# A GRU and an expert-choice layer on one core: the order of the head, and the place of a count in the tail

## The chip, the cores and the metric

The kernel runs on one core of a Trainium2 chip. The metric is the device time of one execution in microseconds (us). Before the change the median of five runs is 1196.7 us (1193.42 to 1199.73).

The engines are named as the profile names them. PE is TensorE (PEld its weight loads), DVE is VectorE, ACT is ScalarE and POOL is GpSimd. SP is SyncE, which issues transfers. SPq, ACTq and POOLq are transfers that these engines issue.

## The reference

`x` is [16, 256, 512]: 16 sequences, 256 steps, 512 features. A GRU runs over the steps from the state `cond_2048`:

```python
def cell(h, x):
    gi = x @ W_ih + b_ih
    gh = h @ W_hh + b_hh
    i_r, i_z, i_n = jnp.split(gi, 3, axis=-1)
    h_r, h_z, h_n = jnp.split(gh, 3, axis=-1)
    r = jax.nn.sigmoid(i_r + h_r)
    z = jax.nn.sigmoid(i_z + h_z)
    n = jnp.tanh(i_n + r * h_n)
    h_new = (1.0 - z) * n + z * h
```

All 4096 states then go through a router with 16 experts. Each expert chooses the 256 tokens with its highest softmax weight; all experts share one matrix.

```python
S = jax.nn.softmax(xf @ router_w + router_b, axis=-1)
G, idx = jax.lax.top_k(S.T, k)               # k = 256 tokens for each expert
out = jnp.einsum('ekh,hd->ekd', xf[idx], expert_w) + expert_b
y = zeros.at[idx.reshape(-1)].add((G[..., None] * out).reshape(-1, h))
```

The result is `x + y`. As the experts share a matrix, a token's `y` is its product with `expert_w` plus `expert_b`, times the sum of its chosen weights, its gate.

## The kernel before

**Sizes and tiles.** The steps come in 32 groups of 8 (`TG`), and a group has four pairs of steps. 512 columns are four chunks of 128 (`KC`). A gate's 512 columns are computed as four quadrants of 32 partitions, so one group of four matmuls fills 128 partitions. A float32 matmul shows as two instructions in the profile.

**The head.** SyncE and ScalarE load the two weight matrices, each by three gates in the order r, n, z and in halves (L229). GpSimd issues, in an order written out by hand: the biases (L274), the x of group 0 into `xa0` (L237, eight transfers of 16 partitions by four pairs), a memset and the start state `cond` (L279, into a part of the tile `xs`). SyncE then loads the x of group 1 into `xa1`, which shares its buffer with `xa0`, and `expert_w`, `router_w` and the two broadcast biases (L284 to L287). Eight transfers of SyncE and ScalarE together are in flight at a time, and eight of GpSimd.

On TensorE, `begin_sums` (L110) writes zero products into a PSUM bank, which opens its sums. There are banks `ra`, `hn` and `zz` for each of two pairs of steps (index 0 and 1). Bias products follow into both sets (L302), and the set of index 1 is copied to SBUF as `bias` and `nb` (L311 to L313), from which later pairs are preset (L384 to L386). VectorE transposes the x of group 0 in one instruction (`turn_x`, L253) and the start state (L316, L321). Then `x_part` (L398) adds the products with `W_ih` for pairs 0 and 1: first r and n of both pairs, then z of both.

**The steps.** For each step, `h_part` (L411) adds the products with `W_hh`: r and n by halves of the depth, then z. ScalarE and VectorE make the new state (L468 to L508). VectorE transposes each new `hs` half by half, and TensorE starts the next step when the first half is there. The order of all engines in the steps is written out by hand. The x products of the next pair (L398) and the expert products of earlier groups (L365) fill TensorE's waits. `turn_x` for the next group is called at the fourth step of a group (L524), and `load_x` and `load_xa` issue x transfers on SyncE behind a small GpSimd copy.

**The late groups.** The odd groups and group 30 are `late_groups`, 17 of them, with eight parts of products each (L138, a part is four matmuls, eight instructions). `expert_for(n)` emits the next n parts on TensorE. A late group's sum is begun two groups ahead: ScalarE presets its PSUM buffer with `expert_b` (L158), and five buffers rotate. Late groups that end before the gate is known are copied to SBUF (L175); the others stay in PSUM until `store`.

**The tail.** Each expert's threshold is found bit by bit on VectorE (`count`, L585, and L600 to L608), with late parts between the count products on TensorE. After 17 bits, an exact selection among the highest eight remaining values (L667 to L684) gives `kth`. Four products (`sum_weights`, L628) give each token's gate, L632. Then 32 `store`s follow (L638, L641): 15 groups whose sums are ready, and then the 17 late groups, each after its parts. After the third store, the kernel counts once more with `kth` (L702 to L707), to learn whether each expert has exactly 256 tokens. If not, a general path is run behind a branch (L709); on these inputs it is not. The order of TensorE, ScalarE and VectorE is by hand here too, so an instruction that waits holds up all that its engine has behind it.

Of the kernel before, what the change touches and what calls it, by code (L numbers as in the profile page):

```python
# [18 lines left out]
def kernel(  # L19
# [166 lines left out]
    with (  # L186
# [63 lines left out]

        def turn_x(g, xa):
            t = xtp.tile([P, TG // 2, P], F32, name="xt")
            nc.vector.transpose(  # L253
                t.rearrange("p q (c r) -> p q c r", c=KC), xa.rearrange("p q (i c) -> p q c i", c=KC)
            )
            xT[g] = t

# [3 lines left out]
        xa1 = new_xa()  # L261
        with tc.manual_schedule(engines={ET.SP, ET.Activation, ET.Pool}):
            for i, gate in enumerate((0, 2, 1)):
                load_rows(wih[:, :, i, :], w_ih[:, gate * D : (gate + 1) * D], "(p c) n -> p c n")
            for gate in (0, 2, 1):
                load_rows(whh[:, :, gate, :], w_hh[:, gate * D : (gate + 1) * D], "(c p) n -> p c n")

            for dst, src in (
                (b_raw[0:1], b_ih.rearrange("(o g d) -> o g d", o=1, d=D)),
                (b_raw[1:2], b_hh.rearrange("(o g d) -> o g d", o=1, d=D)),  # L270
                (b_n, b_hh[2 * D :].rearrange("(o d) -> o d", o=1)),
                (b_r, router_b.rearrange("(o e) -> o e", o=1)),
            ):
                nc.gpsimd.dma_start(out=dst, in_=src)  # L274
            for j in range(KC):
                load_xa(0, xa0, j, (nc.gpsimd, nc.gpsimd))
            nc.gpsimd.memset(c0, 0.0)
            for j in range(KC):
                nc.gpsimd.dma_start(  # L279
                    out=c0[QD * j : QD * j + B, :].rearrange("b (c i) -> b c i", c=KC), in_=columns(cond, j)  # L280
                )
            for j in range(KC):
                load_xa(1, xa1, j, (nc.sync, nc.sync))
# [6 lines left out]

        for i in range(2):
            for bank in (ra[i].rearrange("p g d -> p (g d)"), hn[i], zz[i]):
                begin_sums(bank)
            for dst, rows in (
# [6 lines left out]
                for j in range(KC):  # L301
# [8 lines left out]
                    )  # L310
        nc.vector.tensor_copy(bias[:, 0:2, :], ra[1])  # L311
        nc.vector.tensor_copy(bias[:, 2, :], zz[1])
        nc.vector.tensor_copy(nb, hn[1])  # L313

        turned = gp.tile([P, P], F32, name="nT")
        nc.vector.transpose(turned, c0)  # L316

        def of_step(ap, odd):
            return ap.rearrange("p (c q b) -> p c q b", q=2, b=B)[:, :, odd, :]

        nc.vector.tensor_copy(hs[:, :, 0, :], of_step(turned, 0))  # L321

# [97 lines left out]

        turn_x(0, xa0)
        make_masks()
        xa_next = xa1
        for z in (False, True):
            for p in range(2):
                for k in range(KC):
                    x_part(p, k, z)

# [7 lines left out]
        with tc.manual_schedule(engines={ET.PE, ET.Activation, ET.DVE, ET.Pool, ET.SP}):  # L436
            units = []
            for s in range(T):
# [79 lines left out]
                if odd and p + 2 < T // 2:  # L518
                    preset(p + 2)
                if apart and c == 0:  # L520
                    less_max(g - 1, hn[(p + 1) % 2][:, P:])
# [44 lines left out]
    with (  # L566
# [86 lines left out]
        with tc.manual_schedule(engines={ET.PE, ET.Activation, ET.DVE}):  # L653
# [25 lines left out]
            nc.tensor.matmul(all_most, same_f, spread.rearrange("p h n -> p (h n)"), start=True, stop=True)  # L679
            expert_for(2)  # L680
            room = above(counts)
# [6 lines left out]
            for q in range(QG):  # L688
                part = slice(q * P, (q + 1) * P)
                nc.vector.scalar_tensor_tensor(at_least[:, part], sT[:, part], kth, sT[:, part], ALU.is_ge, ALU.mult)  # L690
                sum_weights(q, pg)
            gate = gate_of(pg)

            gated.append(True)
            for i, g in enumerate([g for g in range(NG) if g not in late_groups] + late_groups):
                while g in late_groups and g not in late_done:
                    expert_for(1)
                store(g, late_sums.get(g, wide(g)), gate)
                if i == 2:

# [93 lines left out]
```

## Time and profile before

| | |
|---|---|
| median of five runs | 1196.7 us |
| the profiled execution | 1194.21 us, its span 1192.4 us |
| mean granted TensorE clock | 0.996 |
| last bias product ends, first x product starts | 11.93, 17.92 us |
| first product of step 0, of step 1 | 24.78, 28.87 us |
| gate sums end, late parts go on | 1144.83, 1148.32 us |
| late parts end | 1186.55 us |

How to read it: times are microseconds from the span's start. In a timeline line stand the start, the time, the engine, the line of the kernel, the operation, the tiles (out, then in), the shapes, the count of instructions put together, and in brackets how long the engine had been idle and what ended this. A line with a count over one can have holes inside. In a line of a window the columns are the stretch and its length, the busy time of PE, PEld, DVE, ACT and POOL with their counts, the granted TensorE clock (1.00 is full), the busy share of the DMA engines, and GB/s. In the head the clock column reads 1.00 throughout, though the first x products (17.9 to 21.3) start every 0.43 us by groups of four and the later ones every 0.22.

### The profile page before, as it was taken

What the parts mean: (1) busy time and instruction counts of PE and PEld (TensorE: products, weight loads), DVE (VectorE), ACT (ScalarE), POOL (GpSimd) and SP (SyncE); (2) the same over time, 40 slices, a digit from 0 to 9 for tenths busy, and PEclk for the clock granted to TensorE, in tenths of its full rate; (3) what the DMA queues carried; (4) which work ended last, traced back from release to release, by engine and by line L of the source; (5) the groups of instructions that cost most, each with busy time, mean ns of one, the idle gap of its engine ahead of it and who ended that gap; (6) DMA issues with size and microseconds to landing.
All of it is one profiled execution on the core that took longest, in us unless ns stands there. A gap on an engine that the chain in (4) does not pass through costs nothing.

```text
span 1192.4 us, 80820 instructions
## 1 busy us (share of the span) xinstructions
PE 1154.9 (97%) x36477; PEld 1047.7 (88%) x36477; DVE 684.9 (57%) x3868; ACT 319.4 (27%) x1430; POOL 99.4 (8%) x412
## 2 busy tenths in 40 slices
PE   5999999999999999999999999999999999999788
PEld 3899999999999999999999999999899999999444
DVE  2555655565565656555565556565565556555682
ACT  0222222223222222222222222222222222223210
POOL 3000000000000000000000000000000000000000
PEclk9999999999999999999999999999999999999999
DMA  8000000000000000000000000000000000000044
GB/s 274 25 23 20 20 18 23 20 20 20 20 20 20 19 21 20 20 20 20 21 20 21 18 20 19 22 19 21 20 20 18 22 20 20 18 14 13 2 144 143
DMA packets 48349, 38.09 MB, mean 32 GB/s; under 512 B 7744, under 2 KB 40064, under 8 KB 48000
## 3 DMA queue, kind: packets, MB, share of 16 engines
q1 hardware_dynamic: 45856, 29.43, 8.5%
q8 instruction: 287, 4.70, 1.6%
q10 hardware_dynamic: 1632, 3.15, 0.8%
q14 instruction: 62, 0.51, 0.1%
q0 software_dynamic: 512, 0.31, 0.1%
HBM read 24.47 MB, written 8.39 MB: 28 GB/s over the span
## 4 chain that ended last, share of the span: by engine, by line
PE 91%; DVE 5%; DMA 1%; issue 1%; ACT 1%; POOL 0%; DVEq 0%; ACTq 0%; POOLq 0%
PE ra L411 19%; PE hn L411 19%; PE ra L398 17%; PE zz L411 17%; PE zz L398 10%; PE pe L365 5%; PE pe L138 4%; DVE nT L494 1%; DVE t L485 1%; DVE zT L497 1%; DVE ge L585 1%; ACT n L489 1%; DMA xs<-in_L_cond_b_hh_dram 1%; DMA xs<-in_cond_dram 0%; DVE hs L508 0%
## 5 line engine op out<-in xcount | busy, mean ns | idle before, releaser
L411 PE MATMUL ra<-whh,hs 128*16 128x128 f32 (+1 forms) x8192 | 345.1, 273 | 7.7 <-DVE zT L497 6.1
L411 PE MATMUL hn<-whh,hs 128*16 128x128 f32 (+1 forms) x8192 | 345.0, 273 | 0.0
L485 DVE TENSOR_TENSOR t<-r,hn 128x64 f32<-128x64 f32 x512 | 90.5, 218 | 360.5 <-PE hn L411 357.0
L398 PE MATMUL ra<-wih,xt 128*32 128x256 f32 x4096 | 286.0, 381 | 7.1 <-DVE xt L253 6.0
L411 PE MATMUL zz<-whh,hs 128*16 128x128 f32 (+1 forms) x8192 | 285.4, 273 | 0.1
L411 PEld LDWEIGHTS ra<-whh,hs 128*16 128x16 f32 (+1 forms) x8192 | 242.7, 103 | 17.7 <-issue 6.8
L411 PEld LDWEIGHTS hn<-whh,hs 128*16 128x16 f32 (+1 forms) x8192 | 256.8, 103 | 0.2
L411 PEld LDWEIGHTS zz<-whh,hs 128*16 128x16 f32 (+1 forms) x8192 | 239.8, 103 | 1.5 <-issue 0.9
L468 ACT ACTIVATE r<-ra 128x128 f32<-128x128 f32 x256 | 71.0, 277 | 595.8 <-PE ra L411 595.8
L398 PEld LDWEIGHTS ra<-wih,xt 128*32 128x32 f32 x4096 | 157.0, 110 | 40.7 <-DVE xt L253 6.4
L489 ACT ACTIVATE n<-t 128x64 f32<-128x64 f32 x512 | 103.5, 249 | 193.1 <-DVE t L487 192.9
L398 PE MATMUL zz<-wih,xt 128*32 128x128 f32 x4096 | 146.1, 273 | 1.0 <-issue 0.9
L398 PEld LDWEIGHTS zz<-wih,xt 128*32 128x32 f32 x4096 | 128.6, 110 | 16.3 <-issue 3.1
L494 DVE STREAM_TRANSPOSE nT<-n 128x64 f32<-128x64 f32 x512 | 100.6, 234 | 57.2 <-ACT n L489 56.8
L497 DVE STREAM_TRANSPOSE zT<-zs 128x64 f32<-128x64 f32 x512 | 121.7, 238 | 0.7 <-ACT zs L490 0.4
L508 DVE TENSOR_TENSOR hs<-v,nT 128x32 f32<-128x32 f32 x512 | 101.8, 199 | 21.7
L505 DVE TENSOR_TENSOR v<-u,zT 128x32 f32<-128x32 f32 x512 | 104.6, 204 | 8.8
L365 PE MATMUL pe<-ewr,ht 128*32 128x136 f32 (+1 forms) x1920 | 107.8, 276 | 0.0
L487 DVE TENSOR_TENSOR t<-t,ra 128x64 f32<-128x64 f32 x512 | 88.6, 214 | 0.1
L365 PEld LDWEIGHTS pe<-ewr,ht 128*32 128x32 f32 x1920 | 75.7, 110 | 10.9 <-issue 0.2
L500 DVE TENSOR_TENSOR u<-hs,nT 128x32 f32<-128x32 f32 x512 | 78.3, 153 | 0.0
L138 PE MATMUL pe<-ewr,ht 128*32 128x256 f32 x1088 | 66.4, 394 | 0.0
(109 smaller groups left out, 494.3 us busy)
## 6 DMA issues: line engine op xcount, KB each, us to landing
xs<-in_x_dram SPq DMA_DIRECT2D x128, 64.0 KB, 2.3
out_dram<-xs SPq DMA_DIRECT2D x32, 256.0 KB, 3.6
xa<-in_x_dram SPq DMA_DIRECT2D x248, 32.0 KB, 1.9
wih<-in_L_cond_W_ih_dram SPq DMA_DIRECT2D x3, 512.0 KB, 8.1
wih<-in_L_cond_W_ih_dram ACTq DMA_DIRECT2D x3, 512.0 KB, 9.0
whh<-in_L_cond_W_hh_dram SPq DMA_DIRECT2D x3, 512.0 KB, 13.8
whh<-in_L_cond_W_hh_dram ACTq DMA_DIRECT2D x3, 512.0 KB, 14.5
ewr<-in_L_ffn_expert_w_dram SPq DMA_DIRECT2D x1, 1024.0 KB, 5.7
```

The lines of the kernel that those rows point to most:

```text
L138: nc.tensor.matmul(pe[q, cols], ht[:, g, k, q], ewr[:, k, E:][:, cols], start=False, stop=(k == KC - 1), tile_position=(0, QD * j), skip_g ...
L365: nc.tensor.matmul(pe[quadrant(j), at : at + w], ht[:, g, k, quadrant(j)], ewr[:, k, src : src + w], start=(k == 0), stop=(k == KC - 1), t ...
L398: nc.tensor.matmul(dst, lhs, rhs, start=False, stop=(k == KC - 1), tile_position=(0, QD * j), skip_group_check=True)
L411: nc.tensor.matmul(dst[quadrant(j, m)], lhs, columns(whh[:, k, gate_, :], j), start=False, stop=(k == KC - 1), tile_position=(0, QD * j), ...
L485: nc.vector.tensor_tensor(t[half], r[:, cols], hn[p % 2][:, cols], ALU.mult)
L487: nc.vector.tensor_tensor(t[half], t[half], ra[p % 2][:, 1, cols], ALU.add)
L489: nc.scalar.activation(n[half], t[half], AF.Tanh)
L494: nc.vector.transpose(nT[half], n[half])
L497: nc.vector.transpose(zT[half], zs[:, halves[half][1]])
L500: nc.vector.tensor_tensor(u[half], hs[:, halves[half][2], slot(s), :], of_step(nT[half], odd), ALU.subtract)
L505: nc.vector.tensor_tensor(v[half], u[half], of_step(zT[half], odd), ALU.mult)
L508: nc.vector.tensor_tensor(hs[:, halves[half][2], slot(s + 1), :], v[half], of_step(nT[half], odd), ALU.add)
```

## The change

*In the head.* The x of group 0 is loaded pair by pair, four transfers of 32 partitions to a pair (`load_pair`). GpSimd issues those of pair 0 ahead of the biases and those of pair 1 behind `cond`; SyncE issues those of pairs 2 and 3 behind the weights and ahead of `xa1`. `turn_x` can transpose some pairs only: pair 0 and pair 1 separately in the head, pairs 2 and 3 together after step 1. On TensorE all sums are begun first, then 22 rounds of zero products go into a spare bank (`keep_clock`), then come the x products of pair 0, two rounds, the biases of both sets, two rounds, and the x products of pair 1. The order of TensorE and VectorE in this stretch is now by hand, with the start state's transpose last on VectorE.

*In the tail.* Three late parts are called earlier: one more after the selection's product, and one after each second gate product. The count for the general path moves from behind the third store to behind that of index 28 (`NG - 4`), the 14th late group; three stores remain after it.

```diff
-        def turn_x(g, xa):
-            t = xtp.tile([P, TG // 2, P], F32, name="xt")
+        def turn_x(g, xa, pairs=slice(0, TG // 2)):
+            if g not in xT:
+                xT[g] = xtp.tile([P, TG // 2, P], F32, name="xt")
             nc.vector.transpose(
-                t.rearrange("p q (c r) -> p q c r", c=KC), xa.rearrange("p q (i c) -> p q c i", c=KC)
-            )
-            xT[g] = t
+                xT[g][:, pairs, :].rearrange("p q (c r) -> p q c r", c=KC),
+                xa[:, pairs, :].rearrange("p q (i c) -> p q c i", c=KC),
+            )
...
+            def load_pair(p, qs):
+                for j in range(KC):
+                    qs[j % 2].dma_start(
+                        out=xa0[quadrant(j), p, :],
+                        in_=x[:, 2 * p : 2 * p + 2, j * P : (j + 1) * P].rearrange("b o d -> o b d"),
+                    )
...
+            load_pair(0, (nc.gpsimd, nc.gpsimd))
             for dst, src in (
...
-            for j in range(KC):
-                load_xa(0, xa0, j, (nc.gpsimd, nc.gpsimd))
             nc.gpsimd.memset(c0, 0.0)
...
+            load_pair(1, (nc.gpsimd, nc.gpsimd))
+            for p in range(2, TG // 2):
+                load_pair(p, (nc.sync, nc.sync))
             for j in range(KC):
                 load_xa(1, xa1, j, (nc.sync, nc.sync))
...
+        idle = ps_m.tile([P, D], F32, name="idle", tag="pe")
+        def keep_clock(n):
+            for _ in range(n):
+                begin_sums(idle)
+
+        with tc.manual_schedule(engines={ET.PE, ET.DVE}):
+            for i in range(2):
+                for bank in (ra[i].rearrange("p g d -> p (g d)"), hn[i], zz[i]):
+                    begin_sums(bank)
+            keep_clock(22)
+            turn_x(0, xa0, slice(0, 1))
+            for z in (False, True):
+                for k in range(KC):
+                    x_part(0, k, z)
+            keep_clock(2)
+            biases(1)
+            biases(0)
+            keep_clock(2)
+            nc.vector.tensor_copy(bias[:, 0:2, :], ra[1])
+            nc.vector.tensor_copy(nb, hn[1])
+            nc.vector.tensor_copy(bias[:, 2, :], zz[1])
+            turn_x(0, xa0, slice(1, 2))
+            for z in (False, True):
+                for k in range(KC):
+                    x_part(1, k, z)
+            nc.vector.transpose(turned, c0)
+            nc.vector.tensor_copy(hs[:, :, 0, :], of_step(turned, 0))
         make_masks()
         xa_next = xa1
-        for z in (False, True):
-            for p in range(2):
-                for k in range(KC):
-                    x_part(p, k, z)
...
+                if s == 1:
+                    turn_x(0, xa0, slice(2, TG // 2))
...
-            expert_for(2)
+            expert_for(3)
             room = above(counts)
...
                 sum_weights(q, pg)
+                if q % 2:
+                    expert_for(1)
...
-                if i == 2:
+                if i == NG - 4:
```

`biases(i)` holds the bias products that stood in a loop before; `begin_sums`, `x_part` and the bias products themselves are unchanged.

## The prediction

> **What bounds the kernel now.** I read the page's busy shares first, then the chain of waits, and then the timeline of the two ends, because the diff touches only the head, the first steps and the tail.
>
> ```profile
> PE 1154.9 (97%) x36477; PEld 1047.7 (88%) x36477; DVE 684.9 (57%) x3868; ACT 319.4 (27%) x1430; POOL 99.4 (8%) x412
> PE 91%; DVE 5%; DMA 1%; issue 1%; ACT 1%; POOL 0%; DVEq 0%; ACTq 0%; POOLq 0%
> ```
>
> The 256 steps between the ends are TensorE's and stay as they are. What can move is the time until TensorE begins step 0, and the holes it has after the last step. The head, from the timeline:
>
> ```profile
> 3.40 2.06 POOL L237 DMA_DIRECT2D xa<-in_x_dram  x4
> 8.08 1.07 PE L302 MATMUL ra<-xs,ones 2*32 2x128 f32 x16 [6.09 <-DMA xs<-in_L_cond_b_hh_dram]
> 11.76 0.51 POOL L279 DMA_DIRECT2D xs<-in_cond_dram  x1
> 16.78 1.08 DVE L253 STREAM_TRANSPOSE xt<-xa 128x512 f32<-128x512 f32 x1 [4.50 <-DMA xs<-in_cond_dram]
> 17.92 5.29 PE L398 MATMUL ra<-wih,xt 128*32 128x256 f32 x64 [5.99 <-DVE xt L253]
> 23.03 1.92 PE L398 MATMUL zz<-wih,xt 128*32 128x128 f32 x64
> 23.67 0.31 SPq L237 DMA_DIRECT2D xa<-in_x_dram  x1
> 24.78 0.61 PE L411 MATMUL ra<-whh,hs 128*16 128x128 f32 x16
> 28.87 0.64 PE L411 MATMUL ra<-whh,hs 128*32 128x128 f32 x16 [1.30 <-DVE zT L497]
> ```
>
> TensorE idles from 11.93 (the last bias product) to 17.92 for the transposed x of group 0, whose transfers GpSimd issues behind the biases. It then needs 7 us for the x products of pairs 0 and 1. The SyncE line at 23.67 dates the last weights: eight of the SyncE and ScalarE transfers are in flight at a time, and by the queue's waits this seventh xa transfer waited for whh's third gate (z), its SyncE half; the ScalarE half had landed by 24.03. The tail:
>
> ```profile
> 1143.65 1.18 PE L628 MATMUL pg<-row_of,at_least 128*128 128x8 f32 x8
> 1147.09 0.74 DVE L585 TENSOR_SCALAR_CACHE_REDUCE ge<-sT,kth 128x512 bf16<-128x512 f32 x1
> 1147.89 0.16 PE L702 MATMUL n<-cnt,same_h 128*128 128x1 f16 x1 [3.06 <-DVE ge L585]
> 1148.32 38.23 PE L138 MATMUL pe<-ewr,ht 128*32 128x256 f32 x680
> 1160.51 2.76 DVE L638 SCALAR_TENSOR_TENSOR xs<-pe,gate,xs 128x512 f32<-128x512 f32 x4
> 1186.68 0.75 DVE L638 SCALAR_TENSOR_TENSOR xs<-pe,gate,xs 128x512 f32<-128x512 f32 x1 [2.70 <-DMA out_dram<-xs]
> ```
>
> TensorE is idle from 1144.83 to 1148.31, but for one count product: the count stands in its order before the remaining 85 late parts (680 instructions), and those end the kernel. The hole also costs clock; the granted clock is the column before the last two:
>
> ```profile
> 1147.00:1148.00 1.00, 0.11 (x1) 0.00 (x0) 0.84 (x3) 0.00 (x0) 0.00 (x0) 0.83 0.80 193
> 1148.00:1151.00 3.00, 2.75 (x30) 1.27 (x33) 2.65 (x6) 0.00 (x0) 0.00 (x0) 0.50 0.57 202
> 1151.00:1152.00 1.00, 1.00 (x24) 0.54 (x20) 1.00 (x3) 0.00 (x0) 0.00 (x0) 0.96 0.92 242
> 1188.50:1189.00 0.50, 0.00 (x0) 0.00 (x0) 0.00 (x0) 0.00 (x0) 0.00 (x0) 0.62 0.67 139
> 31.50:35.00 3.50, 2.25 (x84) 2.04 (x80) 1.66 (x11) 1.52 (x7) 0.17 (x1) 1.00 0.10 27
> ```
>
> Half clock runs from 1147.66 (0.83 over that 1 us) to 1151.08. The late parts lose half of 1148.31 to 1151.08, 1.4 us.
>
> **The head, step by step.** GpSimd's sixteen transfers stay sixteen, at about 0.5 us of issue each and eight in flight. Pair 0's four now go first, 1.33 to 3.4; with the 6.1 us to landing of this queue's xa row they land by 9.0. The transpose of a quarter costs 0.31 (row of the 128x128 turn of c0), so 9.3. wih's gates r and n have landed by 10.31 (that ScalarE issue waited for one), the third by about 13.3, one more interval of 3.3. The 22 zero products are 88 instructions; one group of four 512-wide starts 0.22 us after the other late in the run, 0.43 at half clock, so they end between 7 and 11.4; at worst they delay x by 1 us and this is hidden by what follows. Pair 0's x products are half of 64 and 64 instructions: at full clock 1.75 + 0.88, ending near 14 behind wih's third gate. The biases (3.85 at the slow pace of 8.08 to 11.93) and four more zero products (0.9 to 1.7) then end between 17 and 18.5; the three bias copies (0.42 + 0.31 + 0.29) run beside them.
>
> Pair 1's four transfers take the last four places on GpSimd, where cond was: last issue about 11.8, and with cond's 6.4 landed near 18.1. The memset of c0 moves within this queue; masks wait behind and are wanted late. Turn 0.31: 18.4; c0's turn and copy (0.5) follow on VectorE beside the x products. Those take 2.6: step 0 begins at 21.0 instead of 24.78. Its r and n parts need 4 x 0.44 and end at 22.8. Then z waits for whh: 23.7 to 24.0. From there 0.87 of products, 0.15 to the end of the last, zs 0.26, zT 0.17, v 0.17, hs 0.2 and gaps of 0.1 give step 1 at 26.0 instead of 28.87: **2.9 gained**. Bounds: 3.8 if weights never bind (24.78 - 21.0); 2.1 if pair 1's products meet half clock (1.7 lost). I keep 2.9, as the weights' row is direct.
>
> What else moves: the turn of pairs 2 and 3 (half of 1.08) goes behind step 1 on VectorE, into its idle 33.51 to 35.03, and frees the buffer that xa1 shares. Their eight transfers stand on SyncE behind the weights, the last issued near 24.4 when a place comes free, landed by 28.7 at 4.3; wanted at 30.6. xa1's eight, and then expert_w, router_w, the two broadcasts and the first x loads, now wait on SyncE until that turn, near 31.2. At 0.42 an issue the last xa1 goes at 34.2 and lands by 38.5 at 4.3, by 36 at 1.7; its turn comes at 41.89 - 2.9 = 39.0. Covered, by 0.5 at the least; expert_w is first used after step 8, near 60. The masks' 2 us of VectorE work lie in its wait for step 0 (idle 6.9 before). Zero for these.
>
> The Trainium skill, "DMA: Bandwidth & Descriptors", Rules for kernel authors, speaks against the pair loads: an outermost dimension below 16 confines a DMA to that many engines, and theirs is 2. No row of before shows such a load. As an estimate from that page, 64 KB on each of two engines instead of 8 on each of sixteen would add some 2 us to pairs 2 and 3, and the sum would stay.
>
> **The tail, step by step.** Three late parts of 0.43 go into holes: the third behind all_most moves pg's first product from 1143.65 to 1143.73, the one inside pg moves gate from 1144.87 to 1145.36, and one follows pg. The late parts then run on from 1145.34 instead of 1148.31, 83 of them where 85 stood. VectorE starts its stores at 1145.58 and no longer stops for the count (1147.09 to 1148.59). The next thing late is a PSUM buffer: late group 11 takes that of late group 6, whose sum is VectorE's 22nd store. 21 stores at 0.667 end at 1159.6; that store and ScalarE's copy (0.75 + 0.6) give 1161.0; TensorE would be there at 1145.34 + 35 x 0.4316 = 1160.45, so it waits 0.55. Then 24 parts (10.4) to 1171.4, and the count: store 0.76, count 0.77, products and compare 0.16 + 0.17 + 0.16, with gaps 2.25, in which the 24 parts behind it stand still. 1173.6 + 10.4 = 1184.1 against 1186.55: **2.4 gained** at full clock. The flag is ready 10 us before the end.
>
> That wait of 2.25 can bring half clock back. The rows: after TensorE's end at 1186.55 the clock fell at about 1188.6, 2.06 us idle; 1.25 us idle in 31.5 to 35.0 did not do it. The price is 0 to 1.4 (the row at 1148). The halves of the clock in this trace come on a grid of 3.41 us (21.30, 1147.66, 1151.08, 1188.6), so a wait of 2.25 puts about 2 us into one interval a little more than half the time; I take **0.8**, between the ends.
>
> The rule of "TensorE: Matmul & The Clock Gate", Why this matters for your kernels, in the Trainium skill is that idle gaps up to about 3 us keep the clock. By it the price would be 0 and the time 1191.4; the row at 1188.5 says otherwise.
>
> **Sum.** 2.9 + 2.4 - 0.8 = 4.5 us. The profiled execution took 1194.2 (span 1192.4 and 1.8 around it), so 1189.7 for its like; the median of the runs is 2.5 above it, 1196.7, which gives **1192.2**.
>
> **Rivals.**
> 1. *The weights cover the head.* If whh's z gate lands 2 to 3 us later, because the pair loads share its queues, the head gives 0 to 0.9 and the whole 1.6 to 2.5: about 1195. For it: the z gate is already the last to arrive. Against: no more bytes go before it than now.
> 2. *The moved count costs what it saved.* Half clock for a full 3.41 (1.7) and the buffer wait on top leave 0.7 of the tail: 3.6 in all, 1193.1. For it: the row at 1188.5.
> 3. *Slower: x comes late for the first steps.* Pairs 2 and 3 and then xa1 are two rounds of eight on SyncE, the second chained to the first. At the pace of before's eight (6.56 in all, 4.3 to landing) behind 23.7, pairs 2 and 3 land at 34.5, turn to 35.1: 3.0 lost beyond VectorE's idle time; xa1 lands at 46.0 against 42.0: 4 lost. 7.0 - 4.5 gives 1199.2; it decides from 4.5 us of stall. Against: that pace came from waits for weights, and places free up earlier.
> 4. *The change doesn't do it:* pair 0's turn waits for all of xa0. Then the products begin near 28 and it is some 10 us slower. Against: the bias products began at 8.08 while cond, in the same tile, landed near 18.
>
> **How the numbers follow.** A measurement of this kernel tells about 0.3% (3.6 us) from no change. Forecast 0.65 (1190 to 1194.5, over 3.6 gained in four of five), rival 1 0.16, rival 2 0.08, rival 3 0.08 (half over 0.3%), rival 4 0.03. Faster 0.57, same 0.33, slower 0.10. The low end is 1196.7 less 3.8 + 2.4 and 1 of scatter, 1189.5; the high end takes in rival 1 and part of rival 3, 1197.5.
>
> **What would show it.** Step 0 near 21, step 1 near 26, and z's weights as what step 0 waits for; the page without a wait of VectorE for xa in steps 1 to 4; late parts from 1145.3 on that scale without a break but for 0.5 and 2.2 us; half clock after the count or not. A wait of xt (L253) inside the steps, or z's weights past 25, would make the prediction wrong.

## The result and the profile after

The changed kernel took 1196.39 us in the median of 42 runs, the kernel before 1197.36 in the median of 70 beside it: a ratio of 0.9991, with a 95% interval of 0.9983 to 1.0. By this ratio that is 1.1 us less, somewhere between 0 and 2.0, where 4.5 had been forecast. The profiled execution took 1197.48 us (span 1195.4, mean clock 0.994).

The busy shares, and the first line of the chain of waits, of the kernel after:

```profile
PE 1162.0 (97%) x36581; PEld 1049.4 (88%) x36581; DVE 685.7 (57%) x3870; ACT 320.6 (27%) x1430; POOL 100.7 (8%) x412
...
PE 89%; DVE 6%; DMA 1%; issue 1%; ACT 1%; POOL 0%; DVEq 0%; ACTq 0%; POOLq 0%
```

TensorE still bounds the kernel, and these shares don't show a change. The head has to be read in the timeline of the kernel after:

```profile
1.44 2.52 POOL L267 DMA_DIRECT2D xa<-in_x_dram  x4 [0.57 <-issue]
...
1.77 5.88 PE L114 MATMUL idle<-zero 128*32 128x512 bf16 x88
...
9.06 1.06 POOL L287 DMA_DIRECT2D xs<-in_cond_dram  x2 [2.79 <-DMA xa<-in_x_dram]
11.06 1.02 POOL L287 DMA_DIRECT2D xs<-in_cond_dram  x2 [0.93 <-DMA xa<-in_x_dram]
11.35 0.40 DVE L254 STREAM_TRANSPOSE xt<-xa 128x128 f32<-128x128 f32 x1 [10.46 <-DMA xa<-in_x_dram]
...
11.81 3.64 PE L401 MATMUL ra<-wih,xt 128*32 128x256 f32 x32 [4.16 <-DVE xt L254]
...
12.11 2.41 POOL L267 DMA_DIRECT2D xa<-in_x_dram  x4
...
17.66 0.64 PE L311 MATMUL ra<-xs,ones 2*32 2x128 f32 x16
...
20.27 0.40 DVE L254 STREAM_TRANSPOSE xt<-xa 128x128 f32<-128x128 f32 x1 [1.07 <-DMA xa<-in_x_dram]
...
20.73 3.59 PE L401 MATMUL ra<-wih,xt 128*32 128x256 f32 x32 [0.45 <-DVE xt L254]
...
24.14 1.05 PE L401 MATMUL zz<-wih,xt 128*32 128x128 f32 x32
...
25.02 0.61 PE L414 MATMUL ra<-whh,hs 128*16 128x128 f32 x16
...
29.12 0.64 PE L414 MATMUL ra<-whh,hs 128*32 128x128 f32 x16 [1.31 <-DVE zT L524]
```

The x of pair 0 is turned at 11.35 and its products run from 11.81. In the kernel before no x product ran until 17.92. But pair 1 is turned only at 20.27, its products take from 20.73 to 25.02, and step 0 begins there, 0.24 later than before. Step 1 follows 4.10 behind step 0, as it did before (4.09): no weight is waited for.

The window rows of the same stretch show the granted clock, the column before the last two:

```profile
10.50:17.30 6.80, 5.49 (x68) 3.30 (x72) 0.40 (x1) 1.28 (x1) 4.45 (x11) 0.50 1.06 368
17.30:20.70 3.40, 2.98 (x96) 1.93 (x88) 1.26 (x5) 0.00 (x0) 0.00 (x0) 1.00 1.06 326
20.70:24.10 3.40, 3.37 (x32) 1.58 (x36) 1.72 (x11) 0.00 (x0) 0.30 (x1) 0.50 0.21 68
```

The clock is half where the x products of pair 0 run and half again where those of pair 1 run. It is full between them, where TensorE does the bias products.

The timeline of the tail in the kernel after:

```profile
1149.03 0.61 PE L657 MATMUL pg<-row_of,at_least 128*128 128x8 f32 x4
...
1150.68 15.31 PE L138 MATMUL pe<-ewr,ht 128*32 128x256 f32 x280
...
1166.36 10.57 PE L138 MATMUL pe<-ewr,ht 128*32 128x256 f32 x192 [0.37 <-ACT pe L158]
...
1178.53 0.16 PE L733 MATMUL n<-cnt,same_h 128*128 128x1 f16 x1 [1.60 <-DVE ge L614]
...
1178.96 10.56 PE L138 MATMUL pe<-ewr,ht 128*32 128x256 f32 x192
```

From the first product of pg (L657, 1149.03) to the end of the last late part (1189.52) it is 40.49 us; before it was 42.90, from 1143.65 to 1186.55. The tail gave 2.41. The large hole in front of the late parts is gone. In its place are a wait of 0.37 for ScalarE's preset and, inside a hole of 2.0 us (1176.93 to 1178.96), the count.

Between the head and the tail lie the steps. From the sigmoid of r of step 8 to that of the last step this profile has 1051.42 us and that of before 1046.96, so the profiled execution ends later although the tail is shorter. Nothing of the change is in this stretch; a table behind the experiments takes it up.

### The profile page after: what moved, and what is told of

Its sections match the earlier page's. It is cut to its first block, busy times and chain, and to the rows that moved or that the text cites. A ratio compares the mean times of both kernels' runs of the same rounds, so it can differ in the third digit from the quotient of the medians.

```text
span 1195.4 us, 81045 instructions
## 1 busy us (share of the span) xinstructions
PE 1162.0 (97%) x36581; PEld 1049.4 (88%) x36581; DVE 685.7 (57%) x3870; ACT 320.6 (27%) x1430; POOL 100.7 (8%) x412
## 3 DMA queue, kind: packets, MB, share of 16 engines
q10 hardware_dynamic: 1632, 3.15, 0.8%
## 4 chain that ended last, share of the span: by engine, by line
PE 89%; DVE 6%; DMA 1%; issue 1%; ACT 1%; POOL 0%; DVEq 0%; ACTq 0%; POOLq 0%
PE ra L414 19%; PE hn L414 19%; PE ra L401 17%; PE zz L414 17%; PE zz L401 9%; PE pe L368 5%; PE pe L138 3%; DVE xs L667 1%; DMA xa<-in_x_dram 1%; DVE nT L521 1%; DVE t L512 1%; DVE zT L524 1%; ACT n L516 1%; DVE ge L614 1%; DVE hs L535 0%
## 5 line engine op out<-in xcount | busy, mean ns | idle before, releaser
L414 PE MATMUL ra<-whh,hs 128*16 128x128 f32 (+1 forms) x8192 | 341.0, 273 | 7.9 <-DVE zT L524 6.0
L414 PE MATMUL hn<-whh,hs 128*16 128x128 f32 (+1 forms) x8192 | 339.9, 273 | 0.0
L401 PE MATMUL ra<-wih,xt 128*32 128x256 f32 x4096 | 282.6, 383 | 4.7 <-DVE xt L254 4.6
L414 PEld LDWEIGHTS ra<-whh,hs 128*16 128x16 f32 (+1 forms) x8192 | 238.9, 103 | 19.0 <-issue 8.3
L414 PEld LDWEIGHTS hn<-whh,hs 128*16 128x16 f32 (+1 forms) x8192 | 252.9, 103 | 0.1
L401 PEld LDWEIGHTS ra<-wih,xt 128*32 128x32 f32 x4096 | 154.6, 111 | 38.2 <-DVE xt L254 5.6
L401 PEld LDWEIGHTS zz<-wih,xt 128*32 128x32 f32 x4096 | 127.6, 110 | 19.4 <-issue 5.7
L368 PE MATMUL pe<-ewr,ht 128*32 128x136 f32 (+1 forms) x1920 | 103.4, 276 | 0.0
L368 PEld LDWEIGHTS pe<-ewr,ht 128*32 128x32 f32 x1920 | 72.9, 110 | 11.2
L517 ACT ACTIVATE zs<-zz 128x128 f32<-128x128 f32 x256 | 66.3, 259 | 6.0 <-PE zz L414 5.1
```

Of the source, the lines that this page charges most:

```text
L368: nc.tensor.matmul(pe[quadrant(j), at : at + w], ht[:, g, k, quadrant(j)], ewr[:, k, src : src + w], start=(k == 0), stop=(k == KC - 1), t ...
L401: nc.tensor.matmul(dst, lhs, rhs, start=False, stop=(k == KC - 1), tile_position=(0, QD * j), skip_group_check=True)
L414: nc.tensor.matmul(dst[quadrant(j, m)], lhs, columns(whh[:, k, gate_, :], j), start=False, stop=(k == KC - 1), tile_position=(0, QD * j), ...
```

## The experiments

My theory after reading the two traces: the tail gave what was forecast, and the head gave nothing, because pair 1 landed late and its products met half clock. The rivals: the head is a loss of its own that eats the tail's gain (the steps get longer behind it); the clock fell from idle TensorE alone; the pair loads are slow because GpSimd's queue was crowded, not from their shape.

### Each half alone

The change's tail with the head as it was before (`load_xa` of group 0 behind the biases, one turn of all pairs, no zero products besides those that open the sums), so that only this is left of the change:

```diff
-            expert_for(2)
+            expert_for(3)
...
+                if q % 2:
+                    expert_for(1)
...
-                if i == 2:
+                if i == NG - 4:
```

> The head of before with the tail of the change. My theory (the tail gives what it was priced at, the head gives nothing, and the 256 steps vary from execution to execution by themselves): gate sums to the end of the late parts 2.2 us shorter than before, or 0.8 if the half clock follows the count; time 0.998 to 0.9995 of before; from the first to the last sigmoid of r anything from 1078 to 1086 us. Rival (the change makes the steps longer, and the head is the part that does it): the time is 2.2 us or more under before and the steps take 1080 us as in before's profile.

And the change's head with the old tail, the same three places turned back:

```diff
-            expert_for(3)
+            expert_for(2)
...
-                if q % 2:
-                    expert_for(1)
...
-                if i == NG - 4:
+                if i == 2:
```

> The head of the change with the tail of before. My theory: step 0 begins near 25.0 us as in the change's profile (24.8 before), time 0.9995 to 1.0005 of before; the steps again anything from 1078 to 1086 us. Rival: the steps take near 1085 us, as in the change's profile, and the time is 3 to 5 us over before.

Both ran on one chip, beside the kernel before at 1203.13 us. The tail alone took 1200.27, a ratio of 0.9975 (0.9954 to 0.9995). The head alone took 1205.27, 1.001 (0.9989 to 1.0032). From pg to the end of the late parts the tail alone needed 40.49 us in its profile, to the hundredth what the whole change needed. The head alone began step 0 at 25.42, where the kernel before had 24.78. So the gain is the tail's, and the head is worth nothing that these runs can show; in its profile steps 0 and 1 began 0.6 and 0.7 us later than before.

Both ratios lie 0.0005 outside what was expected (0.998 to 0.9995, and 0.9995 to 1.0005). From the first to the last sigmoid of r it was 1090.3 us with the old head and 1090.75 with the new one, where 1078 to 1086 was expected: long in both, so these two profiles don't speak for the rival of a head that lengthens the steps.

### Why TensorE ran at half clock in the head

Three kernels differ from the change in the zero products of the head. The first has enough of them to fill the wait for pair 0, and more behind the biases:

```diff
-            keep_clock(22)
+            keep_clock(42)
...
-            keep_clock(2)
+            keep_clock(12)
```

> The change with 42 rounds of zero products in place of 22 ahead of pair 0's x products, and 12 in place of 2 behind the biases. My theory (the half clock in both sets of x products is one of two causes of the head's miss, because TensorE goes idle before x arrives and the thin bias products don't keep the clock): pair 0's products at full clock (2.7 us, not 5.2), pair 1's too (2.6, not 4.5), step 0 near 23.2 instead of 25.0, 1.7 us less than the change's head. Rival (the zero products count for nothing, only late x does): step 0 stays at 25.0.

It took 1201.12 us against 1203.13, 0.998 (0.996 to 1.0). The first part came true: the 42 rounds ran to 12.7 without a break, and pair 0's products followed at full clock, 1.90 and 1.05 instead of 3.64 and 1.94. The second did not. The 12 rounds behind the biases themselves ran at half clock (42 of their 48 instructions took 4.06 us from 19.42 on, behind a pause of 0.97), were in the way of pair 1, and step 0 began at 25.70 where 23.2 was expected.

The next one also moves pair 1's loads ahead of the biases on GpSimd, so that its x is there sooner:

```diff
             load_pair(0, (nc.gpsimd, nc.gpsimd))
+            load_pair(1, (nc.gpsimd, nc.gpsimd))
...
-            load_pair(1, (nc.gpsimd, nc.gpsimd))
...
-            keep_clock(22)
+            keep_clock(42)
...
-            keep_clock(2)
+            keep_clock(12)
```

> As the kernel with 42 and 12 rounds of zero products, and pair 1's transfers also go ahead of the biases on GpSimd. My theory (late landing of pair 1 is the other cause): pair 1 lands near 14 instead of 20.2, the biases near 17 and cond near 19; step 0 begins near 21, waits for whh's n gate (21.0) and z gate (23.3), and step 1 begins near 25.5 instead of 29.1; the time is 3.5 us under the change and 4 to 5.5 under before. Rival (whh's weights or cond bind as soon as pair 1 does not): step 1 at 28 or later.

It took 1201.89 us, 0.9991 (0.9971 to 1.0011). Pair 1 was turned at 17.50, and it was of no use: step 1 began at 29.03, in the rival's range and not near 25.5, but neither weights nor `cond` were the cause. The timeline and two windows of this kernel (clock before the last two columns) say why:

```profile
12.27 1.91 PE L401 MATMUL ra<-wih,xt 128*32 128x256 f32 x32
...
16.03 0.64 PE L311 MATMUL ra<-xs,ones 2*32 2x128 f32 x16
...
17.71 0.40 PE L311 MATMUL zz<-xs,ones 2*32 2x128 f32 x8
18.04 4.46 PE L114 MATMUL idle<-zero 128*32 128x512 bf16 x48
22.34 1.90 PE L401 MATMUL ra<-wih,xt 128*32 128x256 f32 x32
```

```profile
18.00:20.00 2.00, 2.00 (x29) 0.90 (x28) 0.43 (x4) 0.00 (x0) 0.00 (x0) 0.57 1.05 378
20.00:22.00 2.00, 2.00 (x28) 0.87 (x24) 1.34 (x8) 0.00 (x0) 0.18 (x1) 0.58 0.58 204
```

From 12.27 on TensorE has work nearly without a break (its longest pause is 0.19 us), and still the clock falls to half at 18.27, behind two microseconds of bias products (16.03 to 18.04). The zero products that should hold the clock then run at half speed, and they stand ahead of pair 1, whose products wait until 22.34 for nothing but them.

A bias product contracts over one or two rows (2\*32 or 1\*32 in its shape), a zero product over 128. The third kernel tries just that: zero products of the same width, contracted over two rows, and 42 rounds of them.

```diff
-                begin_sums(idle)
+                for j in range(KC):
+                    nc.tensor.matmul(
+                        idle[QD * j : QD * (j + 1)],
+                        zero[0:2],
+                        zero[0:2, 0:E].unsqueeze(1).to_broadcast([2, D // E, E]),
+                        start=True,
+                        stop=True,
+                        tile_position=(0, QD * j),
+                    )
...
-            keep_clock(22)
+            keep_clock(42)
```

> The change with 42 rounds of zero products in place of 22, and all of these rounds contract over 2 rows in place of 128, with the same 512 columns. My theory (products over one or two rows, as the bias products are, do not raise or hold the clock): no full clock in the head until some 3.4 us of x products have run, that is not before 15 us; with 128 rows the clock was full from 5.45. Rival (TensorE's time decides, not the rows): full clock from 4 to 7 us on.

In a single run it took 1215.12 us against 1200.82. The timeline of its head:

```profile
1.92 18.10 PE L430 MATMUL idle<-zero 2*32 2x512 bf16 x168
19.95 3.64 PE L401 MATMUL ra<-wih,xt 128*32 128x256 f32 x32
...
25.23 0.61 PE L430 MATMUL idle<-zero 2*32 2x512 bf16 x8
```

168 products ran for 18.1 us without a pause, 0.43 us to a round of four. The same rounds over 128 rows need 0.22 at full clock, and 42 of them had brought full clock by 5.45 in the kernel with more zeros. The x products behind them also began at half speed (3.64 us), and the clock rose only at 25.26, after five microseconds of real products. This settles it: idle time is not needed for half clock. Products over two rows did not raise the clock here in 18 us, and products over one or two rows did not hold it in the run above.

The Trainium skill, "TensorE: Matmul & The Clock Gate", "Part 1: The HAM clock gate", says that about 3.4 us of sustained matmul activity releases the throttle, whatever the number of products. The runs agree for 128 rows (full clock by 5.45, with products from 0.92 on) and disagree for two: here 18.1 us of back-to-back products did not release it.

### Why pair 1 landed late

GpSimd's pair loads take 0.62 us to issue and, by the row of transfers of the kernel after (last number: median us from issue to landing), 6.6 to land:

```profile
xa<-in_x_dram POOLq DMA_DIRECT2D x8, 16.0 KB, 6.6
```

This kernel loads pairs 0 and 1 step by step instead, twice as many transfers of half the size, each with 16 partitions outermost instead of two steps:

```diff
+                    if p < 2:
+                        for o in range(2):
+                            q = QD * j + B * o
+                            qs[o].dma_start(out=xa0[q : q + B, p, :], in_=x[:, 2 * p + o, j * P : (j + 1) * P])
+                        continue
```

> The change with the loads of pairs 0 and 1 cut into transfers of 16 partitions (16 rows outermost, 8 KB), twice as many. If the shape of the pair loads (outermost dimension 2) makes them slow: 0.51 us of issue each in place of 0.62, and 5.7 to 6.5 us from issue to landing for the first ones in place of 7.0 to 8.0. If it is the weights beside them: 7 to 8 us as before. Pair 0 lands near 11 either way (eight issues), step 0 does not begin earlier than 25.

```profile
xa<-in_x_dram POOLq DMA_DIRECT2D x16, 8.0 KB, 5.7
```

The issue fell to 0.49 us and the landing to 5.7, about what this queue had before (0.51, and 6.1 for the xa transfers). So the shape makes a pair load slow, not the number of transfers, of which there were more in this run. Their size is no rival either: before's xa transfers, of 32 KB and with 16 partitions outermost, took those 0.51 and 6.1. The issue time of some 0.6 is the same in every profile. The landing of pair 0 is not: with the same order of loads it was 7.0 to 8.0 in the kernel after, 6.4 in the one with more zeros and 6.5 to 6.7 in the change run again, and 5.5 to 6.2 for the cut loads. Cutting the loads doesn't help the whole, since sixteen issues take longer than eight: pair 1 was turned at 22.63 and step 0 began at 27.71. A single run gave 1204.34 us against 1200.82.

### What a better order is worth

If the two causes are right, the head can be made to gain by an order that avoids both. First the tail, by itself: the count's products are called six late parts behind its VectorE work, so that nothing waits for it.

```diff
-                    nc.tensor.matmul(n, same_h, count(kth, "cnt"), start=True, stop=True)
+                    cnt = count(kth, "cnt")
+                    expert_for(6)
+                    nc.tensor.matmul(n, same_h, cnt, start=True, stop=True)
+                    expert_for(2)
```

> The change with the count's product behind six more late parts, and the product of its compare behind two more, so that TensorE has work while VectorE stores and counts. My theory (the count's place still costs TensorE 2.2 us, and the half clock in some executions): no wait over 0.5 us among the last 24 late parts and no half clock there; from the last sigmoid of r to the end of the late parts 76.0 us, where the change took 77.8 to 79.5; time 2 to 3 us under the change. Rival (VectorE or the stores bind by then): 77.8 or more.

1197.34 us against 1200.82, 0.9969 (0.9953 to 0.9984). The timeline of its tail has the two products of the count (L735, L740) among late parts without a hole:

```profile
1182.23 0.18 PE L735 MATMUL n<-cnt,same_h 128*128 128x1 f16 x1
1182.34 1.07 PE L138 MATMUL pe<-ewr,ht 128*32 128x256 f32 x16
1183.23 0.17 PE L740 MATMUL n_wrong<-wrong 128*1 128x1 f16 x1
1183.23 7.09 PE L138 MATMUL pe<-ewr,ht 128*32 128x256 f32 x128
```

From pg to the end it now takes 38.52 us, 1.97 less than with the change: the stall of the count was worth its 2 us. From the last sigmoid of r to the end of the late parts it is 75.99, as expected.

Then the head, on top of that tail. GpSimd issues the biases first, then pairs 0 and 1, then `cond`. TensorE does the bias products in two short blocks with zero products between and behind them, then pairs 0 and 1:

```diff
-            load_pair(0, (nc.gpsimd, nc.gpsimd))
             for dst, src in (
...
                 nc.gpsimd.dma_start(out=dst, in_=src)
+            load_pair(0, (nc.gpsimd, nc.gpsimd))
+            load_pair(1, (nc.gpsimd, nc.gpsimd))
             nc.gpsimd.memset(c0, 0.0)
...
-            load_pair(1, (nc.gpsimd, nc.gpsimd))
...
-            keep_clock(22)
-            turn_x(0, xa0, slice(0, 1))
-            for z in (False, True):
-                for k in range(KC):
-                    x_part(0, k, z)
-            keep_clock(2)
+            keep_clock(24)
             biases(1)
+            keep_clock(5)
             biases(0)
-            keep_clock(2)
+            keep_clock(8)
...
-            turn_x(0, xa0, slice(1, 2))
-            for z in (False, True):
-                for k in range(KC):
-                    x_part(1, k, z)
+            for p in range(2):
+                turn_x(0, xa0, slice(p, p + 1))
+                for z in (False, True):
+                    for k in range(KC):
+                        x_part(p, k, z)
+                if p == 0:
+                    keep_clock(4)
```

> The tail of the kernel with the later count. In the head GpSimd issues the biases first, then pairs 0 and 1, then cond; TensorE does 24 rounds of zero products, the biases with 5 rounds between and 8 behind, and then the x products of both pairs, 4 rounds between. My theory (late pair 1 and the clock were what kept the head): the biases end near 11.5, pair 0's products run at full clock from 12 to 15.5, pair 1's from 16.5 to 19; step 0 waits for whh's n gate (21.0) and z gate (23.3) and step 1 begins near 25.5, where before had 28.9; time 6 to 8 us under before. Rival (something else holds step 0, such as cond): step 1 at 28 or later, time 4 to 5 us under before from the tail alone.

It took 1194.4 us against 1200.82, 0.9959 (0.9943 to 0.9974). That is 4.9 us less by the ratio and 6.4 by the two medians, where 6 to 8 was expected. The timeline of its head:

```profile
9.22 0.64 PE L311 MATMUL ra<-xs,ones 2*32 2x128 f32 x16
...
10.29 1.27 PE L114 MATMUL idle<-zero 128*32 128x512 bf16 x20
...
11.49 0.64 PE L311 MATMUL ra<-xs,ones 2*32 2x128 f32 x16
...
12.56 2.20 PE L114 MATMUL idle<-zero 128*32 128x512 bf16 x32
...
13.08 0.41 DVE L254 STREAM_TRANSPOSE xt<-xa 128x128 f32<-128x128 f32 x1 [2.31 <-DMA xa<-in_x_dram]
...
14.39 2.10 PE L401 MATMUL ra<-wih,xt 128*32 128x256 f32 x32
...
16.64 0.42 DVE L254 STREAM_TRANSPOSE xt<-xa 128x128 f32<-128x128 f32 x1 [3.15 <-DMA xa<-in_x_dram]
...
25.46 0.64 PE L414 MATMUL ra<-whh,hs 128*32 128x128 f32 x16 [1.28 <-DVE zT L523]
```

The clock is full from 6.13 on and stays so through the steps. Pair 1 is turned at 16.64, and step 1 begins at 25.46: 3.4 earlier than before the change, and 3.7 earlier than after it. With half as many bias products in a block and products over 128 rows between the blocks the clock held, here and in two more profiles below. In all eight profiles that have them in one block behind pair 0 it fell, 0.2 to 3.6 us behind that block's end; in some of these TensorE had also been idle by then.

Only part of this reached the end. The kernel with the later count alone had 0.9969 on this chip, and the two intervals overlap, so what this head adds to that tail is not clear of the noise. By the sigmoid of r of step 8 this kernel was at 58.33, only 1.1 ahead of the kernel before at 59.43. TensorE paused for 1.87 us (42.92 to 44.79) without a wait that the profile names. By the count from step 0 used here this is in step 5; the expectations below call it step 4. Ahead of the pause `expert_w`, 1 MB, had been loading: it was issued at 35.34, its semaphore's last step came at 41.77, and from 38 to 42 the DMA engines were 0.91 busy.

### Where that pause comes from

Three more kernels ran on one chip. The first is the one above with `expert_w` and the three loads behind it ahead of group 1's x on SyncE. The second is the one above again, and the third the change itself again.

```diff
-            for j in range(KC):
-                load_xa(1, xa1, j, (nc.sync, nc.sync))
             nc.sync.dma_start(out=ewr[:, :, E:], in_=expert_w.rearrange("(c p) n -> p c n", c=KC))
...
+            for j in range(KC):
+                load_xa(1, xa1, j, (nc.sync, nc.sync))
```

> The head with the biases ahead of the pairs, and now the load of expert_w (1 MB) with the three after it goes out on SyncE ahead of the eight transfers of group 1 of x instead of behind them. In the run with the biases first, step 1 began 3.4 us sooner than in the kernel after the change, but a pause of 1.87 us in step 4 (42.92 to 44.79) fell where expert_w filled the DMA queues, and by r of step 8 only 1.1 us were left against the kernel before (58.33 against 59.43). Theory (the load of expert_w holds up what TensorE is fed with): expert_w is issued near 24 as in the kernel before, where it lay ahead of the steps' first such pause; no pause over 1 us in steps 3 to 5, r of step 8 at 56.3 to 56.9, and the time 1.5 to 2 us under the run with the biases first beside it. Rival (the pauses come by chance, wherever the load is): a pause of this size is missing in the profile of the run with the biases first taken again, or is here too at another step, r of step 8 lies anywhere from 56.5 to 58.5 in both, and the times of the two are within 0.3%.

> The kernel with the biases first and the later count once more, on this chip. If its gain is the kernel's own, the ratio to the kernel before comes out near 0.9959 again, within 0.9943 to 0.9974; if it was the chip's or the draw's, within 0.3% of 1. In its profile the theory of the load has a pause of more than 1 us in steps 3 to 5 again (42.92 to 44.79 the first time), and step 1 at 25.4 to 25.6; the rival of chance has none, or elsewhere.

> The changed kernel itself once more, on the same chip as the two others. My reading: the head gains nothing and the later count 2.0 to 2.3 us, so 0.998 to 0.999 of the kernel before. If its head does cost steps (the profile of the changed kernel had 4.5 us more between r of step 8 and the last r than the profile of before), the stretch is again 4 us over that of the kernels beside it and the time is 1.0 to 1.003; by chance alone the three kernels of this call have this stretch within 1050 to 1058 in no order of their heads.

| kernel | us | ratio to before at 1200.54, 95% |
|---|---|---|
| weights ahead of xa1 | 1193.63 | 0.9948 (0.9931 to 0.9965) |
| biases first, again | 1193.75 | 0.995 (0.9931 to 0.9968) |
| the change, again | 1200.67 | 1.0001 (0.9982 to 1.002) |

The gain of the kernel with the biases first and the later count holds: 0.9959 and 0.995 on two chips, and it beats both the kernel before and the change. The change once more shows nothing; 0.998 to 0.999 was expected.

The pause, in the timelines of TensorE: with the biases first, the first time,

```profile
42.50 0.42 PE L414 MATMUL hn<-whh,hs 128*32 128x128 f32 x7
44.79 0.49 PE L414 MATMUL hn<-whh,hs 128*32 128x128 f32 x9 [1.87 <-issue]
```

the same kernel again,

```profile
42.69 0.42 PE L414 MATMUL hn<-whh,hs 128*32 128x128 f32 x7
43.67 0.49 PE L414 MATMUL hn<-whh,hs 128*32 128x128 f32 x9 [0.56 <-issue]
```

and with the weights ahead:

```profile
29.78 0.27 PE L414 MATMUL hn<-whh,hs 128*16 128x128 f32 x1
31.10 0.52 PE L414 MATMUL hn<-whh,hs 128*16 128x128 f32 x12 [1.05 <-issue]
```

Twice it is the same instruction, the eighth of a block of sixteen in step 5, with 1.87 and 0.56 us. With the load of `expert_w` issued at 24.25 instead of 35.05 to 35.34, the pause is gone from step 5 and one of 1.05 us stands in step 2. The two kernels took the same time, and r of step 8 came at 57.35 and 57.22, as the rival of chance had it. But the place is not chance: it is the same twice, and it moved when the load was moved.

The traces show what TensorE stands for. It has 73139 to 73588 instructions, and one queue brings its instructions in 287 to 289 packets of 16 KB, so a packet holds 256. Between 26 and 1100 us the thirteen profiles have 157 pauses of TensorE of over 0.2 us that end without a named wait (`issue` in the brackets). Counted in the order of their starts, all 157 stand at one of the same two places of each 256 instructions, and all end 1.21 to 1.60 us behind the end of a packet. At the other packets TensorE doesn't pass this place sooner either: 1.19 us behind the packet's end is the least in any profile. So in these pauses, the one above among them, TensorE waits for its next instructions.

Why a packet comes late is shown less well. Around the pause the packets started 6 to 7 us apart in both profiles with the biases first (35.45, then 41.43; 35.23, then 42.34), and 8 with the weights ahead (20.79, then 28.74), where some 4 is usual, and each time `expert_w` was loading in between. That its load holds up the fetch fits this, but no run takes the load away, and in the kernel before a spacing of 6.5 us (24.73 to 31.21) beside the same load caused no pause.

### Are the steps longer?

In the profile of the change, the steps from 8 to the last took 4.5 us more than in the profile before. The change run again also had 3.3 and 5.9 us more than the two kernels beside it, and its 1.0001 lies where that rival put it (1.0 to 1.003). The rival, that the new head makes the steps slower, was therefore not to be dismissed. The table gives that stretch for one profiled execution each, how far this execution lay from the median of its kernel's runs, and the difference of the two, an estimate of the stretch in a median run:

| kernel | steps 8 to last | above its median | difference |
|---|---|---|---|
| before | 1046.96 | -3.15 | 1050.1 |
| after | 1051.42 | 1.09 | 1050.3 |
| tail alone (old head) | 1057.23 | 2.70 | 1054.5 |
| head alone | 1057.07 | 2.14 | 1054.9 |
| more zeros | 1056.95 | 2.52 | 1054.4 |
| pair 1 early | 1054.17 | -0.38 | 1054.6 |
| count later | 1053.81 | 0.70 | 1053.1 |
| biases first | 1050.02 | -2.31 | 1052.3 |
| weights ahead | 1048.53 | -5.16 | 1053.7 |
| biases first, again | 1051.11 | -1.83 | 1052.9 |
| the change, again | 1054.43 | -0.45 | 1054.9 |

The old head with the new tail has the longest steps of the table, and the estimates of before and after are 0.2 apart. The four of one chip (rows 3 to 6), the old head among them, lie within 0.5. On the two other chips (rows 7 and 8, and 9 to 11) the kernels with the biases first lie 0.8 to 2.0 under the change's head beside them.

Laid side by side, 31 of these steps are over 0.2 us longer in the profile after (by up to 1.15) and 21 in the profile before (by up to 0.74). Most of the spread is the wait for instructions. Take TensorE's instructions by 256s again: over these steps the eight places with those named above took 8.9 to 18.4 us more than eight places elsewhere did on average (before 9.4, after 12.1). Without this the stretch is 1037.6 to 1041.8 us in all thirteen profiles, where it is 1047.0 to 1058.0 with it. The two profiles with the old head are the lowest of the thirteen then (1037.6 before, 1038.8 with the tail alone; after 1039.3), so an effect of the new head of some 2 us isn't excluded.

## Why the prediction was wrong

**The step that failed** is the landing of pair 1: "last issue about 11.8, and with cond's 6.4 landed near 18.1". It landed at 20.15. The 6.4 held (6.2 from the last issue at 13.9); the issue was 2.1 late. I had carried over 0.5 of issue and 6.1 to landing from before's xa transfers to loads of another shape. They took 0.62 and 7.0 to 8.0 for pair 0, and GpSimd waited twice, 2.79 and 0.93 (before: 1.83 and 0.43), for its eight in flight before it could go on with `cond`. In the five other profiles with this order of loads the last issue came at 12.5 to 14.0 and the landing at 19.4 to 20.1. In the change run again pair 0 landed within 6.5 to 6.7, and pair 1 was as late (20.05), with 2.31 of waiting for pair 0 and 1.31 for a bias load. How the 2.1 divide between the shape and the place in the queue is not shown: no run changes the shape alone.

**The second** is "Those take 2.6: step 0 begins at 21.0". At half clock they took 4.3. The bound for that, 2.1 instead of 2.9, was in the text, but as an alternative to the weights' wait, and not on top of a late landing. Together the two make the 4.0 us from 21.0 to 25.02: 2.3 until the first product and 1.7 in the products. What I had not seen is that the bias products let the clock fall.

**Right, or without effect:** pair 0 was later than said (turned at 11.35, not 9.3) and its products ran at half clock. This cost nothing, as the run with more zeros shows: there they ran at full clock, and pair 1 was turned at 20.18 all the same. The biases and the zero products behind them were later too (to 20.3 where 17 to 18.5 was forecast). z's weights landed at 22.98 and 23.30 by their semaphores (before 23.02 and 23.66, not the 23.7 to 24.0 that I had read off the queue), and step 0 didn't wait for them. With the biases first, step 0 began at 20.99 and step 1 at 25.46, where the forecast's chain had 21.0 and 26.0: the head that I priced at 2.9 exists, in another order, as far as step 1.

**A cost put at zero:** step 2, ahead of which pairs 2 and 3 are turned. These three lines of VectorE in the kernel after show it:

```profile
33.94 0.67 DVE L254 STREAM_TRANSPOSE xt<-xa 128x256 f32<-128x256 f32 x1 [0.18 <-issue]
...
35.28 0.35 DVE L512 TENSOR_TENSOR t<-r,hn 128x64 f32<-128x64 f32 x2 [0.67 <-PE hn L414]
35.78 0.35 DVE L514 TENSOR_TENSOR t<-t,ra 128x64 f32<-128x64 f32 x2
```

From r of step 2 to r of step 3 it took 4.41 us instead of 4.18: 0.23 lost, the same in every kernel with the new head but the one with half loads (0.41). The turn's own time didn't cost this: VectorE stood idle for 0.67 behind it, as forecast, and the first t came in time. The loss is between the two t's (0.50 from start to start, 0.27 in step 1), in the half loads ahead of the first t, and in all eleven profiles with the new head at the 64th instruction that the profile has of VectorE. What holds that instruction up is not shown.

Rival 3's late x did not come. The first two of the SyncE pair loads took 7.7 and 7.2 us to landing by their semaphores, the last four 2.3 to 2.7; before's xa transfers had 3.2 to 5.6. In their semaphore only two steps came at the end (21.72 and 22.13 for the first of them), behind one at 15.69, right after the issue. That agrees with the Trainium skill, "DMA: Bandwidth & Descriptors", "Why a DMA increments its semaphore by 16 and not by 1", by which a load with two outermost is done by two engines and the rest of the count is written at once.

**The tail was right**: 2.41 measured for 2.4 forecast, the wait for ScalarE 0.37 for 0.55, the hole of the count 2.0 for 2.25. Its clock price was sized at 0.8, between 0 and 1.4. Of the seven profiles with the change's place for the count, five had none of it (40.49 us from pg to the end) and two had 1.68 (42.17), above my upper end, a mean of 0.5. The old place isn't of one price either: 42.90 in the kernel before and 44.49 in the head alone, whose clock was half for twice as long.

**The sum** of what was found is 2.41 for the tail less 0.5, 0.25 for step 1 and 0.23 for step 2: 1.4 us, or 0.9988, within the measured interval. It is an estimate from single profiles. The outcome is rival 1's, a head that gives nothing, by another mechanism than its own: not weights that landed late, but x that landed late and met half clock.

## What to carry to other kernels

A transfer that is moved and given another shape at once has no row in the old profile. Its issue time, its landing time and the transfers in flight have to be bounded anew, and chained: here 0.1 us on each issue and up to 2 us of landing stood in one queue with a limit of eight in flight, and pair 1 landed 2 us late. Zero products over 128 rows brought TensorE's clock up and products over one or two rows neither brought nor held it (nothing in between was tried), so count thin products as idle when you forecast the clock. And where two late things stand on one path, add their bounds instead of choosing between them.

## What the runs showed of the hardware

- Products over two rows, back to back for 18.1 us, left the clock at half. Bias products over one or two rows let it fall at 18.27, with TensorE busy nearly throughout from 12.27.
- A GpSimd load with two steps outermost took 0.62 us to issue and 6.6 in the median to land; the same bytes in two loads with 16 outermost took 0.49 each and 5.7.
- TensorE's instructions come in packets of 256. All 157 pauses of over 0.2 us without a named wait stand at the same place of a packet and end 1.21 to 1.60 us behind a packet's end. The longest, 1.87 us, came behind a load of 1 MB; with that load moved it was gone from there.
- The time of one kernel varies by several us between executions: the change itself ran from 1190.13 to 1201.96 us in 42 runs.
